# Smaller closings and openings between the attention steps of a four-layer fp32 kernel on one Trainium2 core

## The chip, the cores and the metric

The kernel runs on one core of a Trainium2 chip. The metric is the device time of one execution in microseconds; lower is better. A core has five engines with an instruction queue each: TensorE (PE in the profile; its weight loads are PEld), VectorE (DVE), ScalarE (ACT), GpSimd (POOL) and SyncE (SP), which here only issues DMAs. They work side by side and wait for each other through semaphores. Matmul results go to PSUM, which has eight banks of 512 fp32 values for each of 128 partitions.

## What is computed

The input x is (4, 64, 64, 64) in fp32: four images of 4096 tokens with 64 channels. Four layers follow each other, each with a residual:

```python
# layer 0: self-attention over the 4096 tokens
attn = softmax(q @ k.T); x = gamma * (attn.T @ v) + x
# layer 1: layer norm, 1x1 convolutions, depthwise 3x3, gating, channel attention
# layer 2: attention between the 64 rows of the first spatial axis read as
xf = x.reshape(B, 64, 4096)
scores = einsum('bci,bcj->bij', xf, xf)          # 4096 x 4096, symmetric
out = einsum('bcj,bij->bci', xf, softmax(scores)) + x
# layer 3: non-local block with inner width 32
f = softmax(theta(x) @ phi(x).T); y = f @ g(x)
w_y = y @ w_W + w_b
x = x + gamma * (w_y - mean) * rsqrt(var + eps) + beta   # over all images
```

In layers 0, 2 and 3 each score matrix is 4096 x 4096 for each image, so almost all of the work is matmuls and exponentials.

## The kernel before, in words

x stays in SBUF as the tile `X`, [128, 4 images, 2048]. The program is one list of `items`; `run()` walks it and emits after each item what has become due: `at(i, fn)` puts a function behind item i, and two lanes of generators, `conv` (layer 1) and `misc` (loads, closings, openings), move on as `tick(us)` credits them with time; the number that a generator yields is what it costs its lane. Nothing is scheduled at run time: the engines' queues have the order in which the program emits.

The order of the stages: layer 0 of images 0 to 3 with layer 1 in the `conv` lane; then layer 2 of image 0; then, in turn, layer 2 of image 1, layer 3 of image 0, layer 2 of image 2, layer 3 of image 1, layer 2 of image 3, layer 3 of image 2, layer 3 of image 3.

*PSUM.* In layer 2 `new_ps` hands out slots of two banks (0, 1 and 2 in turn), and `new_acc` the accumulators in banks 6 and 7. In layer 3 `take_banks(7)` lets seven banks go round one at a time; the eighth holds the sum of the products. `new_ps` takes two neighbouring banks there and skips one at the wrap. Scores (L1643) take four of them for each item.

*Layer 2 of image 0* (`layer2`, 32 items) computes all scores. `close2` (L1369-1380) divides by the softmax's sums and adds to X: for each of 4 parts a multiplication (L1377) and an addition (L1379) on VectorE.

*Layer 2 of images 1 to 3* (`layer2s`, 72 items, the "diagonal steps") uses the symmetry. A step `n` computes a block pair of scores (L1432, 8 matmuls), its exponentials (L1437) and the products of a step two back (L1484, 8 matmuls), accumulated in two banks for the block `h` (the order is 7, 0, 1, ... 6) and added to `A` in SBUF (`add_to`, L1474). Blocks off the diagonal are also turned (L1449, a transpose on VectorE), summed by columns on POOL (L1460), and multiplied (`turned_products`, L1500, 128 matmuls into two slots). `weights` sends the rows of x that these need (L1415). `close2s` (L1545-1569) closes such an image in five steps: the sums (L1550-1556), then 4 parts, each with 8 transposes of 128x128 blocks of A (L1561) into one two-bank slot, a multiplication by the reciprocal sums (L1562, 128x1024) and two additions to X (L1568, 128x512 each).

*features2* (L1292-1305) writes the layout `ko` for layer 2's scores: in two groups, 8 transposes (L1300) into one slot, two copies by VectorE and ScalarE (L1303), and a DMA for the other half of the partitions after each (L1304).

*Layer 3* (`open3`, `keys3`, `layer3`). `open3` projects X to theta (L1588), phi (L1599) and g (L1607), each in one two-bank slot, with VectorE adding the biases (L1592, L1603, L1609). `keys3` spreads phi over the partitions by 16 DMAs of SP (L1622). `layer3` has 64 items for each image (two halves `nb` of 32 `mc`): scores L1643, exponentials L1654 in two instructions or more (first bank 0, then banks 1 to 3 as far as they are neighbours), products L1700 two items later. The sums of e over mc are made on VectorE (L1691), and for the eight `mc` in `BY_DMA` by accumulating DMAs of POOL (L1671/L1673), into the tile xn. Four or five items after a half `totals` sums over partitions (L1712) and eleven after it `close` projects (L1750).

*Who closes whom.* Image 0's closing is in the `misc` lane from step 2 of layer 2 of image 1. The closing of images 1 and 2 is at steps 8, 12, 22, 32 and 42 of the next image's layer 2, and the opening of image b-1's layer 3 from step 46. features2 of the next image is in the `misc` lane from item 3 of layer 3 (images 0 and 1). Image 3's closing, opening and keys are in the `misc` lane from item 8 of image 2's layer 3.

Of the kernel before, what the change touches and what calls it, by code (L numbers as in the profile page):

```python
# [691 lines left out]
def fast_path(ctx: ExitStack, tc: tile.TileContext, a: dict, out: bass.AP, bad):  # L692
    nc = tc.nc
# [41 lines left out]

    def take_slots(*slots):
        turn_of["slots"], turn_of["ps"], turn_of["banks"] = list(slots), 0, 0
# [144 lines left out]
    sel4 = const.tile([128, 32], F32, name="sel4")  # L882
    pwb = const.tile([128, 2, 2], F32, name="pwb")
# [22 lines left out]
    def setup():  # L906
# [33 lines left out]
        for i in range(4):  # L940
# [5 lines left out]
            yield 4.0  # L946
        nc.vector.tensor_add(sel4, ident[:, 0:32], ident[:, 32:64])
# [345 lines left out]
    def features2(b):  # L1293
# [3 lines left out]
        for g in range(2):  # L1297
            ps = new_ps()
            for i in range(8):
                nc.tensor.transpose(ps[:, bass.ts(i, 128)], x[:, bass.ts(8 * g + i, 128)], ident)  # L1300
            for e, copy in enumerate((nc.vector.tensor_copy, nc.scalar.copy)):
                own, other = slice(64 * e, 64 * e + 64), slice(64 - 64 * e, 128 - 64 * e)
                copy(kv[own, bass.ts(g, 8), e, :], ps[own, :].rearrange("p (a n) -> p a n", n=128))  # L1303
                nc.sync.dma_start(out=kv[other, bass.ts(g, 8), e, :], in_=kv[own, bass.ts(g, 8), e, :])  # L1304
            yield 7.0

    def layer2(b):
# [7 lines left out]
        def scores(n):  # L1315
# [3 lines left out]
            for jb in range(4 * (n % 8), 4 * (n % 8) + 4):  # L1319
# [13 lines left out]
                conv.tick(2.3)  # L1333
# [53 lines left out]
    def layer2s(b, when_free):  # L1387
# [7 lines left out]
        for h in (7, 0, 1, 2, 3, 4, 5, 6):  # L1395
# [3 lines left out]
                for pi, pair in enumerate(SIDES[h]) for gi, g in enumerate(sorted(pair)) for u in range(2)  # L1399
            ]  # L1400
            steps += other + own if h == 6 else own + other
        st = {"e": {}, "T": {}, "esum": {}}

# [38 lines left out]
        def turned(n):  # L1442
# [3 lines left out]
            if ti == 0 and pi not in st["T"]:  # L1446
                st["T"][pi] = new_big("turned")
            T = st["T"][pi].rearrange("p (e s j) -> p s e j", e=16, s=8)
# [4 lines left out]
        def column_sums(n):  # L1453
# [7 lines left out]
            if (pi, ti) == (1, 3):  # L1461
# [30 lines left out]
        def turned_products(h, pi):  # L1492
            T, slots = st["T"][pi], [new_ps(), new_ps()]
# [11 lines left out]
            for i in range(2):  # L1505
                for gi, g in enumerate(sorted(SIDES[h][pi])):
# [11 lines left out]
        def item(n):  # L1518
            h = steps[n][0]
            if n >= 4 and steps[n - 4][0] == h and (n == 4 or steps[n - 5][0] != h):  # L1520
                weights(h)
# [11 lines left out]
            if n - 2 in last_of:  # L1533
                turned_products(*last_of[n - 2])
                if last_of[n - 2] == (6, 0):
                    when_free()
            if n - 5 in last_of and last_of[n - 5][1] == 1:
# [7 lines left out]
    def close2s(b):  # L1545
        x, m = X[:, b], im[b]
        ps = new_ps()
# [3 lines left out]
        tot = sums2[:, b, :]  # L1551
# [5 lines left out]
        yield 2.0  # L1557
        for i in range(4):
            ps, t = new_ps(), new_t()
            for j in range(8):  # L1560
                nc.tensor.transpose(ps[:, bass.ts(j, 128)], m.A[:, 1024 * i + 128 * j : 1024 * i + 128 * j + 128], ident)  # L1561
            nc.vector.tensor_mul(  # L1562
                t.rearrange("p (j n) -> p j n", n=128), ps.rearrange("p (j n) -> p j n", n=128),
                rz[:, bass.ts(i, 8)].unsqueeze(2).to_broadcast([128, 8, 128]),
            )
            xs = x[:, bass.ts(i, 512)].rearrange("p (j h) -> p j h", h=H)
            for o in range(2):
                nc.vector.tensor_add(xs, xs, t.rearrange("p (j o h) -> p j o h", j=8, o=2)[:, :, o, :])  # L1568
            yield 3.0
# [5 lines left out]
    small = {}  # L1575
    held = []

    def open3(b):
# [4 lines left out]
        ps = new_ps()  # L1583
        for nb in range(2):
            for jj in range(2):
                for s in range(2):
                    k = 2 * s + jj
                    mm(  # L1588
                        ps[32 * k : 32 * k + 32, bass.ts(nb, 512)], thw[64 * s : 64 * s + 64, :],
                        tok(x, s, 2 * nb + jj), start=True, stop=True,  # L1590
                    )
        nc.vector.tensor_scalar_add(m.th, ps, V("L3_conv_theta_b"))  # L1592
        yield 3.5

        ps, own = new_ps(), m.tg[:, 2048:3072].rearrange("p (s n) -> p s n", s=2)
        m.own = own
        for j in range(4):
            for s in range(2):
# [456 lines left out]
```

## Time and profile before

| what | us |
|---|---|
| median of 3 runs | 2469.98 |
| lowest, highest | 2468.93, 2474.80 |
| profiled execution: its own time | 2475.64 |
| profiled execution: its span | 2473.9 |
| PE matmul busy | 2431.5 |
| ACT busy | 1642.7 |
| DVE busy | 1428.7 |
| POOL busy | 506.8 |

The granted clock of TensorE was 0.996 of full speed. The stages that the change touches begin at about: layer 2 of image 0 at 1037, layer 2 of image 1 at 1274, layer 3 of image 0 at 1474, layer 2 of image 2 at 1618, layer 3 of image 1 at 1812, layer 2 of image 3 at 1953, layer 3 of image 2 at 2143, layer 3 of image 3 at 2290.

TensorE's longest waits, as the view of waits gives them for the whole span (what waits, for whom, us in total, how often, the longest):

```profile
PE PS L1484 <- DVE A L1474: 6.1, 1, 6.1
PE PS L1643 <- DVE A L1474: 3.3, 3, 1.5
PE PS L1643 <- ACT e L1654: 2.9, 2, 2.5
```

In a timeline a line has the start, the duration, the engine, the line of the program, the operation, output and input, shapes, and the number of records; what stands in brackets is the time that the engine was idle before, and who ended it. A matmul in fp32 of full weights has two records. Busy time of PE is modelled from starts, and neighbouring groups overlap by a tenth of a microsecond; start to start is the safer reading.

### The profile page before, as it was taken

How to read it: one execution, taken by the hardware profiler on the slowest of the kernel's cores; microseconds unless marked ns; L12 is line 12 of the kernel's file. 1: busy time of each engine (PE TensorE's matmuls, PEld its weight loads, DVE VectorE, ACT ScalarE, POOL GpSimd, SP SyncE). 2: the span in 40 equal slices, each digit the busy share in tenths (PEclk: the TensorE clock that was granted, in tenths of full speed). 3: DMA queues.
4: the chain of work that ended last, by engine and by line, in shares of the span. 5: the costliest groups of instructions: out<-in, count | busy, mean ns of one | idle time of the engine just before them, and what ended most of it. 6: DMA issues, size and time to landing. Idle time of an engine off the chain costs nothing.

```text
span 2473.9 us, 62215 instructions
## 1 busy us (share of the span) xinstructions
PE 2431.5 (98%) x27037; PEld 925.5 (37%) x27037; DVE 1428.7 (58%) x1701; ACT 1642.7 (66%) x2979; POOL 506.8 (20%) x345
## 2 busy tenths in 40 slices
PE   9999999999999999999989999999999999999998
PEld 3343453336433643344324442134431244421123
DVE  2010277228822782267335558877668876687886
ACT  4666766667666766666645459954479744569996
POOL 2000000000000000000007661256631366512110
PEclk9999999999999999999999999999999999999999
DMA  3000000010000000000000027610075400376554
GB/s 79 1 18 1 18 1 18 18 19 1 18 18 18 1 18 18 18 2 18 18 18 19 19 48 151 138 27 21 18 148 116 81 21 22 73 139 127 118 118 119
DMA packets 59151, 115.33 MB, mean 47 GB/s; under 512 B 11149, under 2 KB 30326, under 8 KB 58870
## 3 DMA queue, kind: packets, MB, share of 16 engines
q0 software_dynamic: 19136, 67.68, 13.7%
q1 hardware_dynamic: 38981, 41.75, 7.5%
q8 instruction: 214, 3.51, 0.6%
q10 hardware_dynamic: 752, 1.85, 0.2%
q14 instruction: 68, 0.55, 0.1%
HBM read 4.80 MB, written 4.19 MB: 4 GB/s over the span
## 4 chain that ended last, share of the span: by engine, by line
PE 88%; DVE 5%; ACT 4%; DMA 1%; issue 1%; SPq 0%; POOL 0%; DVEq 0%; ACTq 0%; POOLq 0%
PE PS L1116 18%; PE PS L1090 17%; PE PS L1643 8%; PE PS L1700 8%; PE PS L1432 7%; PE PS L1484 7%; PE PS L1500 6%; PE PS L1323 4%; PE PS L1343 4%; PE PS L1200 2%; DVE tg L1691 2%; ACT e L1654 2%; DMA xn<-e 1%; ACT e L1095 1%; PE PS L1165 1%
## 5 line engine op out<-in xcount | busy, mean ns | idle before, releaser
L1095 ACT ACTIVATE e<-PS 128x1024 f32<-128x1024 f32 x512 | 523.7, 1023 | 331.3 <-PE PS L1090 299.2
L1116 PE MATMUL PS<-e,vq 64*64 64x512 f32 x4096 | 573.8, 591 | 0.0
L1090 PE MATMUL PS<-X,q 64*64 64x512 f32 x4096 | 571.6, 591 | 1.8 <-DVE X L974 1.7
L1654 ACT ACTIVATE e<-PS 128x512 f32<-128x512 f32 (+2 forms) x593 | 500.4, 915 | 66.9 <-PE PS L1643 42.8
L1437 ACT ACTIVATE e<-PS 128x512 f32<-128x512 f32 x432 | 253.5, 594 | 289.6 <-PE PS L1432 270.9
L1691 DVE TENSOR_TENSOR tg<-tg,e 128x2048 f32<-128x2048 f32 x174 | 398.6, 2291 | 49.4 <-ACT e L1654 37.0
L1233 DVE SCALAR_TENSOR_TENSOR y<-pad,vec,y 128x1024 f32<-128x1024 f32 x240 | 308.1, 1284 | 7.5
L1460 POOL TENSOR_TENSOR esum<-esum,e 128x1024 f32<-128x1024 f32 x126 | 298.9, 2372 | 58.6 <-ACT e L1437 51.5
L1643 PE MATMUL PS<-tg,ph 32*64 32x512 f32 x4096 | 300.3, 615 | 6.5 <-DVE A L1474 3.3
L1090 PEld LDWEIGHTS PS<-X,q 64*64 64x64 f32 x4096 | 184.4, 133 | 257.3 <-issue 178.8
L1116 PEld LDWEIGHTS PS<-e,vq 64*64 64x64 f32 x4096 | 184.6, 133 | 251.3 <-issue 152.9
L1700 PE MATMUL PS<-e,tg 128*32 128x512 f32 x2048 | 273.5, 606 | 0.0
L1449 DVE STREAM_TRANSPOSE turned<-e 128x1024 f32<-128x1024 f32 x168 | 206.7, 1239 | 79.8 <-ACT e L1437 79.7
L1484 PE MATMUL PS<-e,X 64*64 64x512 f32 x1728 | 232.7, 594 | 6.2 <-DVE A L1474 6.1
L1432 PE MATMUL PS<-ko 64*64 64x512 f32 x1728 | 235.4, 598 | 0.0
L1528 POOL MEMSET A<- 128x4096 f32 x3 | 11.2, 3736 | 1012.5 <-PE PS L1116 1012.5
L1103 DVE TENSOR_REDUCE sums<-zs 128x1 f32<-128x4 f32 x128 | 19.6, 153 | 301.3 <-ACT e L1095 300.9
L1331 ACT ACTIVATE e<-PS 128x1024 f32<-128x1024 f32 x128 | 129.6, 1023 | 83.7 <-PE PS L1323 80.4
L1500 PE MATMUL PS<-turned,xn 32*64 32x256 f32 x5376 | 157.2, 377 | 2.5 <-DVE sums L1554 1.6
L1673 POOL DMA_DIRECT2D xn<-e x112 | 97.6, 906 | 294.4 <-ACT e L1654 201.1
L1474 DVE TENSOR_TENSOR A<-PS,A 128x256 f32<-128x256 f32 (+1 forms) x216 | 92.5, 477 | 105.2 <-PE PS L1500 80.7
L1643 PEld LDWEIGHTS PS<-tg,ph 32*64 32x64 f32 x4096 | 65.4, 130 | 227.7 <-ACT e L1654 175.8
(224 smaller groups left out, 1927.4 us busy)
## 6 DMA issues: line engine op xcount, KB each, us to landing
xn<-e POOLq DMA_DIRECT2D x128, 512.0 KB, 5.3
xn<-X SPq DMA_DIRECT2D x336, 32.0 KB
xn<-t SPq DMA_DIRECT2D x64, 128.0 KB
ph<-tg SPq DMA_DIRECT2D x64, 128.0 KB
ko<-ko SPq DMA_DIRECT2D x16, 256.0 KB
xr<-in_x_dram SPq DMA_DIRECT2D x13, 256.0 KB
q<-q SPq DMA_DIRECT2D x12, 256.0 KB
out_dram<-o SPq DMA_DIRECT2D x7, 256.0 KB
```

What stands on the lines that cost most here:

```text
L1090: mm(ps[64 * c : 64 * c + 64, bass.ts(r, 512)], m.q[rows_, 128 * t + 64 * c : 128 * t + 64 * c + 64], x[rows_, bass.ts(g, 512)], start=Tru ...
L1095: act(es[g // 2][:, bass.ts(g % 2, 1024)], ps, AF.Exp, bias=SHIFT0, accum_out=zs[:, g : g + 1],)
L1116: ins = mm(PS[64 * s : 64 * s + 64, 2048 + 512 * j : 2560 + 512 * j], vq[rows_, :], es[j // 2][rows_, k : k + 512], start=t == 0 and i < 2 ...
L1233: stt(y1, win, wt, y1, ALU.mult, ALU.add)
L1432: mm(ps[64 * c : 64 * c + 64, bass.ts(r, 512)], m.ko[rows_, k : k + 64], m.ko[rows_, bass.ts(h, 512)], start=True, stop=True,)
L1460: nc.gpsimd.tensor_add(esum, st["e"][n - 1] if (pi, ti) == (0, 1) else esum, st["e"][n])
L1484: mm(st["acc"][r][64 * c : 64 * c + 64, :], xw[rows_, jb, :], st["e"][n][rows_, bass.ts(c, 512)], start=n == mine[0], stop=n == mine[-1],)
L1500: mm(slots[q // 2][64 * c : 64 * c + 64, o : o + 256], st["xr"][rows_, w : w + 64], T[rows_, bass.ts(e, 256)], start=e < 2, stop=e >= 14,)
L1643: mm(PS[64 * c : 64 * c + 64, bass.ts(banks[k], 512)], m.ph[32 * k : 32 * k + 32, 128 * mc + 64 * c : 128 * mc + 64 * c + 64], m.th[32 * k ...
L1654: act(e[:, 512 * lo : 512 * k], PS[:, 512 * banks[lo] : 512 * banks[lo] + 512 * (k - lo)], AF.Exp,)
L1691: nc.vector.tensor_add(esum, esum, e)
L1700: mm(st["y"][32 * k : 32 * k + 32, :], m.gx[:, i % 32, :], es[i][:, bass.ts(k, 512)], start=mc == 0, stop=i % 32 == 31,)
```

## The change

It has seven parts.

1. `piece()` hands out one bank in layer 3. Elsewhere it takes a whole slot and returns its first half.
2. A constant `fold2` (128x64) is two identities of 64 on top of each other. In `close2s` a part is now 8 fp32 matmuls, each with a 128x128 block of A as weights and fold2 as the moving operand, in one bank, followed by 8 fused multiply-adds of 128x64 on VectorE (`stt`: PSUM times the reciprocal sum, plus X). The transposes, the multiplication and the two additions go, and so does the tile `t`.
3. Image 0's closing moves from the `misc` lane at step 2 to steps 12, 13, 22 and 23 of layer 2 of image 1.
4. features2 has 4 pieces of 4 transposes, with half-sized copies and DMAs, twice as many.
5. open3 has 6 one-bank pieces: theta split by half, phi by `s`, g by 8 tokens' groups.
6. `between3` holds what is emitted in layer 3 right after the exponentials of an item: features2 at items 4, 7, 10 and 13; image 3's closing and opening at items 6, 8, ... 26 of image 2's layer 3; its `keys3` behind item 25; `totals` and `close`, except at the end of a half with n = 63 of images 0 and 1. In such an item the exponentials are cut at bank 2 instead of bank 1.
7. In `layer2s`, `weights` of a block is emitted one step before the block begins, T is chosen by a running index, and pairs are taken as `SIDES` gives them. In layer 2 of image 0 `conv.tick` is 2.5 instead of 2.3.

```diff
+    def piece():
+        if turn_of["banks"]:
+            return PS[:, bass.ts(new_bank(), 512)]
+        return new_ps()[:, 0:512]
...
+        nc.vector.tensor_add(fold2, ident[:, 0:64], ident[:, 64:128])
...
-        for g in range(2):
-            ps = new_ps()
-            for i in range(8):
+        for g in range(4):
+            ps = piece()
+            for i in range(4):
...
-                conv.tick(2.3)
+                conv.tick(2.5)
...
         for i in range(4):
-            ps, t = new_ps(), new_t()
+            ps = piece()
             for j in range(8):
-                nc.tensor.transpose(ps[:, bass.ts(j, 128)], m.A[:, 1024 * i + 128 * j : 1024 * i + 128 * j + 128], ident)
-            nc.vector.tensor_mul(
-                t.rearrange("p (j n) -> p j n", n=128), ps.rearrange("p (j n) -> p j n", n=128),
-                rz[:, bass.ts(i, 8)].unsqueeze(2).to_broadcast([128, 8, 128]),
-            )
-            xs = x[:, bass.ts(i, 512)].rearrange("p (j h) -> p j h", h=H)
-            for o in range(2):
-                nc.vector.tensor_add(xs, xs, t.rearrange("p (j o h) -> p j o h", j=8, o=2)[:, :, o, :])
-            yield 3.0
+                c = 1024 * i + 128 * j
+                mm(ps[:, bass.ts(j, 64)], m.A[:, c : c + 128], fold2, start=True, stop=True)
+            for j in range(8):
+                xs = x[:, bass.ts(8 * i + j, 64)]
+                stt(xs, ps[:, bass.ts(j, 64)], rz[:, 8 * i + j : 8 * i + j + 1], xs, ALU.mult, ALU.add)
+            yield
...
-        for j in range(4):
+        for s in range(2):
+            ps = piece()
+            for j in range(4):
+                mm(
+                    ps[32 * j : 32 * j + 32, :], phw[64 * s : 64 * s + 64, :],
+                    tok(x, s, j), start=True, stop=True,
+                )
+            nc.vector.tensor_scalar_add(own[:, s, :], ps, V("L3_conv_phi_b"))
+            yield 3.0
+        for i in range(2):
+            ps = piece()
+            for t in range(8):
+                mm(ps[:, bass.ts(t, 64)], x[:, bass.ts(8 * i + t, 128)], gw, start=True, stop=True)
...
-            exp(0, 1)
+            cut = 2 if first + n in between3 else 1
+            exp(0, cut)
             if mc == 1 and (nb or last):
                 held.append(lambda: exp(1, 4))
             else:
-                exp(1, 4)
+                exp(cut, 4)
+            for fn in between3.get(first + n, []):
+                fn()
...
-                misc_from[f + 2] = [close2(0)]
+                turns = close2(0)
+                for i in (12, 13, 22, 23):
+                    at(f + i, lambda turns=turns: next(turns))
...
-                misc_from[f + 3] = [features2(b + 1)]
+                turns = features2(b + 1)
+                for i in (4, 7, 10, 13):
+                    between3[f + i] = [lambda turns=turns: next(turns)]
...
-    def keys_of_last():
-        keys3(B - 1)
-        yield 3.5
-
-    misc_from[f - 56] = [close2s(B - 1), open3(B - 1), keys_of_last()]
+    ends = [close2s(B - 1)] * 5 + [open3(B - 1)] * 6
+    for i, gen in enumerate(ends):
+        between3[f - 58 + 2 * i] = [lambda gen=gen: next(gen)]
+    at(f - 39, lambda: keys3(B - 1))
```

## The prediction

> **What bounds the kernel now.** I read the page's head first, then the busy time of each engine stage by stage, then TensorE's timeline at the places that the diff touches. The page's head and the shares of the chain of waits:
>
> ```profile
> span 2473.9 us, 62215 instructions
> PE 2431.5 (98%) x27037; PEld 925.5 (37%) x27037; DVE 1428.7 (58%) x1701; ACT 1642.7 (66%) x2979; POOL 506.8 (20%) x345
> PE 88%; DVE 5%; ACT 4%; DMA 1%; issue 1%; SPq 0%; POOL 0%; DVEq 0%; ACTq 0%; POOLq 0%
> ```
>
> TensorE is busy for 2431.5 of 2473.9 us. The view by stretches says the same of the stages that the change touches (us of the stretch, then PE's busy time):
>
> ```profile
> 1290.00:1478.00 188.00, 182.39 (x2976) 86.02 (x2984) 112.21 (x145) 85.46 (x266) 124.23 (x56) 0.98 0.12 30
> 1618.00:1812.00 194.00, 191.79 (x3056) 89.97 (x3048) 130.03 (x166) 92.20 (x287) 125.26 (x56) 1.00 0.13 30
> 2147.00:2290.00 143.00, 139.58 (x1516) 33.41 (x1520) 112.92 (x72) 114.58 (x141) 26.67 (x32) 0.98 0.66 131
> 2290.00:2430.00 140.00, 138.76 (x1609) 27.43 (x1593) 120.16 (x64) 132.00 (x161) 26.64 (x32) 1.00 0.62 124
> ```
>
> These are layer 2 of images 1 and 2, then layer 3 of images 2 and 3. So the sum has two kinds of terms: instructions added to TensorE (each costs its own time) and moments at which TensorE stands still. Two stages hold visible loss. Layer 2 of image 1 is the one with 5.6 us of idle PE and a clock of 0.98; the timeline of its start shows why:
>
> ```profile
> 1286.95 1.04 PE L1432 MATMUL PS<-ko 64*64 64x512 f32 x8
> 1289.39 2.34 POOL L1460 TENSOR_TENSOR esum<-e 128x1024 f32<-128x1024 f32 x1 [256.40 <-ACT e L1437]
> 1289.56 2.71 DVE L1379 TENSOR_TENSOR X<-X,ph 128x512 f32<-128x512 f32 x1
> 1292.19 1.23 DVE L1449 STREAM_TRANSPOSE turned<-e 128x1024 f32<-128x1024 f32 x1
> 1293.36 1.44 DVE L1474 TENSOR_TENSOR A<-PS,A 128x512 f32<-128x512 f32 x2
> 1294.06 4.48 PE L1484 MATMUL PS<-e,X 64*64 64x512 f32 x16 [6.07 <-DVE A L1474]
> 1297.53 2.19 PE L1432 MATMUL PS<-ko 64*64 64x512 f32 x8
> ```
>
> VectorE was still in image 0's closing (L1377/L1379, back to back since 1284.85) when the accumulators had to be added to A (L1474). TensorE waits 6.07 us for them, and the matmuls after it take twice their time: 4.48 us where 16 of them take 1.90, and 2.19 where 8 take 1.04.
>
> Layer 3 of image 2 carries image 3's closing and opening. TensorE's timeline there:
>
> ```profile
> 2163.64 1.09 PE L1561 MATMUL PS<-ident,A 128*128 128x128 f32 x8
> 2175.44 2.31 PE L1643 MATMUL PS<-tg,ph 32*64 32x512 f32 x16
> 2192.52 3.79 PE L1607 MATMUL PS<-gw,X 128*128 128x64 f32 x32
> 2197.23 1.11 PE L1643 MATMUL PS<-tg,ph 32*64 32x512 f32 x16
> 2224.69 1.98 PE L1643 MATMUL PS<-tg,ph 32*64 32x512 f32 x6 [2.48 <-ACT e L1654]
> ```
>
> The scores of an item take 1.11 us; the 2.31 at 2175.44 means that they waited inside for a bank. And in layer 2 of image 3, where image 2's opening stands between steps:
>
> ```profile
> 1737.69 1.04 PE L1484 MATMUL PS<-e,X 64*64 64x512 f32 x8
> 1738.66 1.09 PE L1599 MATMUL PS<-X,phw 64*32 64x512 f32 x16
> 1739.68 1.09 PE L1432 MATMUL PS<-ko 64*64 64x512 f32 x8
> 1740.59 1.04 PE L1484 MATMUL PS<-e,X 64*64 64x512 f32 x8
> ```
>
> Start to start, the phi matmuls (L1599) take 1.02 there.
>
> **What the Trainium skill says.** "TensorEngine Tiling (Array Packing)", Key Properties: changing the tiling mode drains TensorE. The trace agrees: score to product is 0.86 us start to start, but 0.97 before such an insertion and 0.91 after it (the lines above), so a switch there and back is 0.16. "TensorE: Matmul & The Clock Gate", Terms: the transpose mode is four times faster for fp32; and under LDWEIGHTS, a weight load's time goes with its columns. The trace shows transposes of 128x128 at 0.128 us each (L1561, 8 in 1.02) and fp32 matmuls with 128-column weights and 64 moving columns at 0.2325 (L1607, 16 in 3.72; by the groups its weight loads are busy for 14.6 us in the four images, 3.65 each): not four times, but the second kind does cost more. The same page, "What's actually happening": an idle window of some 3.4 us drops the clock to half. Here 6.07 and 2.48 us of idle PE were followed by doubled matmuls. "SBUF — State Buffer", "SBUF: two separate sides": VectorE with two SBUF inputs and GpSimd lock each other out. The trace agrees: L1379 takes 0.69 alone and 2.71 beside POOL's L1460.
>
> **The change, part by part** (against the profiled execution's span).
>
> *Fold instead of transposes (layer 2 of images 2 and 3).* Each of 4 parts: 8 transposes, 1.02 us, become 8 fp32 matmuls with the A block as 128x128 weights and 64 moving columns. The nearest row is L1607: 8 x 0.2325 = 1.86. That is +0.84 a part; TensorE has no other slack, so 8 parts give +6.7. Bounds: +6.0 (matmuls overlap somewhat better) to +8.5 (the slot, one of three in layer 2, is held by VectorE longer). VectorE: before 1.22 + 2 x 0.69 to 0.935; after 8 fused operations of 128x64, whose nearest rows take 0.21 to 0.29 each, so 1.8 to 2.3. Nothing gained or lost there, since TensorE bounds and the next part comes 10 items later.
>
> *Image 0's closing moved to items 12, 13, 22, 23.* The 6.07 us of idle and the half clock at 1294 go, except that the A add still comes after the first turn (L1449) of the fourth step: at the same place in image 2, 1.17 us went from score to product instead of 0.91, with another matmul covering 1.0 of it. So some 1.5 to 2.1 us of waiting stay. Lost now: 6.07 + 2.5 = 8.6 (the 2.5 is what the slow matmuls took beyond their own time). I take -6.3, with -4 to -8.6. At the new places the pieces (1.4 us each alone) fall around block 0's adds to A (four in 1.42 us); VectorE is busy there for 112 of 188 us, and TensorE notices a late add only when the bank it frees comes round again.
>
> *open3 in six one-bank pieces, in layer 2 of images 1, 2 and 3.* In layer 2 a "bank" is still a whole slot of three. L1588: 8 matmuls in two rounds, 1.86, same work. L1599: 8 matmuls in one round, 1.02; split by s only one of the two row halves works at a time, so two pieces of 1.02: +1.02. One more mode switch, 0.16, for each of phi and the g part, and a wait for a slot of about 0.2. Sum +1.5 for each image, +4.5; 3 to 7.
>
> *features2 in pieces of 4.* In layer 0 and in layer 2 of image 0: two more mode switches each, some +0.4 and +0.4. In layer 3 (images 0 and 1): 8 transposes of 1.02 become two of about 0.55 each; the two stalls of 0.5 and 0.2 us at the old insertions, where the scores waited for the copies, shrink, but there are four places. +0.8 over both, -1.5 to +3. SP gets 8 DMAs of half the size instead of 4; SP has little queued there and ko is needed only 140 us later: nothing.
>
> *Image 3 in layer 3 of image 2.* Before: from 2161.40 to 2197.23 are 11 items, 35.83 us, of which 11 x 2.04 = 22.44 is the items' own; 13.4 on top: matmuls 11.3 and bank stalls 2.1. Then keys3's DMAs, which SP sends from about 2191, met the accumulating DMAs of mc 17, 20 and 23 (9 to 10.5 us instead of 5.3):
>
> ```profile
> ACT e L1654 <- DMA xn<-e: 5.7, 2, 3.9
> ```
>
> ACT waited 5.7 us for them, PE 0.39 and 2.48, and four groups at half clock: 8.0 us in all. Together 21.4. After: matmuls 0.35 + 4 x 1.86 + 2.04 + 2 x 1.02 + 2 x 1.86 = 15.6, one bank each, at every second item, with the exp of that item cut into two halves; stalls of some 0.2 at each of 11 places = 2.2. keys3's DMAs start when the second phi piece is done (item 22, not 18), so that only mc 23 still meets them; one late transfer holds one of the six e buffers, where three held three, and I count nothing. 17.8 - 21.4 = -3.6. Bounds: -8 (no stalls, mode switches hidden) to +2 (the collision costs 6 us still).
>
> *Totals and close between the exps; conv.tick 2.5; weights issued a step earlier in the program; T's index.* Instruction order on POOL and SP is the same, on ACT and DVE nearly; the waits that bound totals (ACT's held exp) stay. 0, -2 to +1.
>
> Sum: 0.8 + 6.7 - 6.3 + 4.5 + 0.8 - 3.6 + 0 = +2.9. The profiled execution took 2475.64 us, 1.7 more than its span of 2473.9, and would become 2478.5; it lies 5.7 above the median of the runs, 2469.98, so the forecast on the median's footing is 2472.9.
>
> **Rivals.**
> (a) *Both losses vanish whole and the fold overlaps.* Start of image 1 -8.6, layer 3 of image 2 -8, features2 -1.5, totals -2, fold only +6, open3 +3, the small +0.8: -10.3, so 2459.7. For it: the losses are measured. Against it: the fold is bound by weight loads (L1607's loads take 3.65 of 3.72), and slots still rotate among three. 0.15.
> (b) *Slower: TensorE's added work and held slots in layer 2.* Everything there stands on the path: fold +8.5, open3 +7, the start of image 1 only -4, layer 3 of image 2 -1, the small terms +2: +12.5, so 2482.5. It decides from the point at which VectorE's eight small operations keep a slot for more than the 2.6 us in which the scores come back to it; they then delay TensorE at each of 8 + 18 insertions by half a microsecond. For it: 98% of PE is busy, so nothing hides work. Against it: VectorE is at 60%. 0.33.
> (c) *The collision moves with the keys.* As forecast, but keys3 at item 22 meets mc 23 and mc 2 of the next half: +6, so 2478.9. Its chance is inside (b).
> (d) *The change doesn't do what it says*, the closing meets POOL's adds at its new place as well and waits 2.71 us a piece: TensorE waits again, -2 instead of -6.3, 2477.2. Inside the forecast's range.
>
> **How the numbers follow.** The forecast, 2472.9, has 0.52; (a) 0.15; (b) with (c) 0.33. The range goes from 2463 to 2484: the forecast's own range, 2465 to 2480, and (b) as well as the upper half of (a). A measurement of this kernel tells about 0.3%, 7.4 us, from no change: under 2462.6 is faster, over 2477.4 slower. Of the forecast's cases nearly all fall in between, of (a)'s most are faster, of (b)'s nine in ten slower: 0.14, 0.52, 0.34.
>
> **What would show it.** The fold's eight matmuls at 1.86 a part in layer 2, or else the price was wrong. At the start of image 1 PE's wait before the first products: about 2 us and no doubled matmuls. The phi pieces at 1.02 each. In layer 3 of image 2 matmuls of 15.6 us and no wait of ACT for xn. If PE's busy sum rises by less than 12 us or the stalls at one-bank insertions exceed 0.5 us each, the sum is wrong.

## The result: 0.5% slower

| | kernel before | changed kernel |
|---|---|---|
| median, us | 2473.57 (6 runs, 2468.93 to 2474.80) | 2484.61 (6 runs, 2484.30 to 2485.78) |
| profiled execution: its time | 2475.64 | 2484.51 |
| profiled execution: its span | 2473.9 | 2482.7 |

The ratio is 1.005, with a 95% interval of [1.0037, 1.0063]. The forecast was 2472.9 with a range to 2484.0; the measured time is above that range, near rival (b)'s 2482.5, but not for (b)'s reason. The forecast stood on 2469.98, the median of three runs of the kernel before; with six runs this median is 2473.57, so 3.6 us of the distance belong to the baseline and not to the change. Against the six runs the change cost 11.0 us where +2.9 was forecast.

The head of the page of the changed kernel, and the shares of its chain of waits:

```profile
span 2482.7 us, 62533 instructions
PE 2444.4 (98%) x27133; PEld 930.9 (37%) x27133; DVE 1416.1 (57%) x1786; ACT 1643.9 (66%) x2980; POOL 507.3 (20%) x345
PE 89%; DVE 5%; ACT 4%; issue 1%; DMA 0%; DVEq 0%; SPq 0%; ACTq 0%
```

TensorE is as full as before, with 12.9 us more of busy time. A table by stage tells where the time went. A stage runs from the first score of its layer and image to the first score of the next stage, in the order of the program; the times are read from TensorE's timelines.

| stage | before | changed | difference | forecast |
|---|---|---|---|---|
| layers 0 and 1 | 1016.47 | 1017.24 | +0.8 | +0.4 |
| layer 2, image 0 | 257.80 | 262.55 | +4.75 | +0.4 |
| layer 2, image 1 | 199.55 | 191.96 | -7.6 | -4.8 |
| layer 3, image 0 | 137.60 | 137.90 | +0.3 | +0.4 |
| layer 2, image 2 | 197.10 | 202.13 | +5.03 | +4.85 |
| layer 3, image 1 | 137.98 | 137.90 | -0.1 | +0.4 |
| layer 2, image 3 | 197.10 | 202.13 | +5.03 | +4.85 |
| layer 3, image 2 | 156.31 | 157.29 | +1.0 | -3.6 |
| layer 3, image 3, and the end | 173.95 | 173.64 | -0.3 | 0 |

Two rows are far worse than forecast: layer 2 of image 0 by 4.35 us, and layer 3 of image 2 by 4.6. Layer 2 of image 1 is 2.8 us better, of which 1.9 is work that moved from there into layer 2 of image 0 (see the run with features2 and the tick undone). The rest is within 0.5 us. Together that makes the 6.0 us by which the profiled execution missed its forecast.

One stage also differs between executions of the same code: layer 2 of image 1 took 191.96 us here and in one other run, and 193.65 in three others that don't touch it. The last section shows why.

TensorE's waits in layer 3 of image 2, in the changed kernel (who waits for whom, us in total, how often, the longest); the kernel before had 2.9 us there for ScalarE, none for tg:

```profile
PE PS L1725 <- DVE tg L1704: 3.4, 1, 3.4
PE PS L1653 <- DVE A L1485: 0.9, 1, 0.9
```

and its timeline at that wait, which is at `totals` of the first half:

```profile
2241.29 1.57 PE L1653 MATMUL PS<-tg,ph 32*64 32x512 f32 x16
2246.27 1.94 PE L1725 MATMUL PS<-tg,ones 128*32 128x512 f32 x8 [3.41 <-DVE tg L1704]
2247.95 1.96 PE L1713 MATMUL PS<-e,tg 128*32 128x512 f32 x8
2249.84 1.95 PE L1653 MATMUL PS<-tg,ph 32*64 32x512 f32 x16
2251.72 1.06 PE L1713 MATMUL PS<-e,tg 128*32 128x512 f32 x8
```

The three groups after the wait take 1.9 us instead of 1.07 to 1.11, and the granted clock says the same. In the view by stretches the second number is the length in us and the third from the right, in front of the DMA's two, the clock:

```profile
2244.77:2251.60 6.83, 5.33 (x32) 1.01 (x32) 4.52 (x4) 0.20 (x1) 0.00 (x0) 0.50 0.35 136
2251.60:2254.00 2.40, 2.40 (x36) 0.55 (x32) 2.21 (x2) 2.17 (x4) 0.00 (x0) 1.00 0.00 0
```

Before, the wait of ScalarE for xn cost TensorE time in this stage; now TensorE waits for VectorE. VectorE's timeline in the changed kernel shows where it becomes late:

```profile
2212.66 2.28 DVE L1704 TENSOR_TENSOR tg<-tg,e 128x2048 f32<-128x2048 f32 x1
2218.05 0.75 DVE L1619 TENSOR_TENSOR tg<-PS,bc_L_conv_g_b 128x256 f32<-128x256 f32 x2 [3.11 <-ACT e L1664]
2218.73 2.28 DVE L1704 TENSOR_TENSOR tg<-tg,e 128x2048 f32<-128x2048 f32 x1
2224.06 0.75 DVE L1619 TENSOR_TENSOR tg<-PS,bc_L_conv_g_b 128x256 f32<-128x256 f32 x2 [3.06 <-ACT e L1664]
2224.74 9.47 DVE L1704 TENSOR_TENSOR tg<-tg,e 128x2048 f32<-128x2048 f32 x4
2234.24 2.29 DVE L1706 TENSOR_TENSOR tg<-tg,xn 128x2048 f32<-128x2048 f32 x1
2236.64 9.48 DVE L1704 TENSOR_TENSOR tg<-tg,e 128x2048 f32<-128x2048 f32 x4
```

Twice VectorE stands idle for 3.1 us at a bias addition of the g pieces (L1619, items 24 and 26), although the sum addition queued behind it (L1704) has its e. The brackets name ScalarE, but g's matmuls on TensorE, which the addition reads, end at nearly the same moment: those of item 26 run from 2221.96 to 2223.96, and ScalarE's exponential of that item ends at 2224.06. Which of the two came last is not told apart here. Either way the bias addition waits for work of its own item, and the sum addition behind it, which could run, waits with it. The addition for mc 24 starts 3.8 us after the scores of item 26; in layer 3 of image 1, with nothing inserted there, the same addition starts 1.0 us ahead of them. After mc 24 no time is made good. Eight additions of 2.37 us start to start and one of xn follow without gaps, and TensorE needs only 2.04 us for an item. L1725 starts at 2246.27, as soon as the last addition is done.

### The profile page after: what moved, and what is told of

Its sections match the earlier page's. It is cut to its first block, busy times and chain, and to the rows that moved or that the text cites. A ratio compares the mean times of both kernels' runs of the same rounds, so it can differ in the third digit from the quotient of the medians.

```text
span 2482.7 us, 62533 instructions
## 1 busy us (share of the span) xinstructions
PE 2444.4 (98%) x27133; PEld 930.9 (37%) x27133; DVE 1416.1 (57%) x1786; ACT 1643.9 (66%) x2980; POOL 507.3 (20%) x345
## 4 chain that ended last, share of the span: by engine, by line
PE 89%; DVE 5%; ACT 4%; issue 1%; DMA 0%; DVEq 0%; SPq 0%; ACTq 0%
PE PS L1123 17%; PE PS L1097 17%; PE PS L1653 9%; PE PS L1713 8%; PE PS L1442 7%; PE PS L1495 7%; PE PS L1511 6%; PE PS L1350 4%; PE PS L1330 4%; DVE tg L1704 3%; PE PS L1207 2%; ACT e L1664 2%; PE PS L1574 1%; ACT e L1102 1%; PE PS L1172 1%
## 5 line engine op out<-in xcount | busy, mean ns | idle before, releaser
L1704 DVE TENSOR_TENSOR tg<-tg,e 128x2048 f32<-128x2048 f32 x174 | 398.4, 2289 | 42.9 <-ACT e L1664 31.4
L1653 PE MATMUL PS<-tg,ph 32*64 32x512 f32 x4096 | 295.3, 614 | 2.8 <-DVE A L1485 2.7
L1460 DVE STREAM_TRANSPOSE turned<-e 128x1024 f32<-128x1024 f32 x168 | 206.6, 1238 | 86.3 <-ACT e L1447 86.3
L1511 PE MATMUL PS<-turned,xn 32*64 32x256 f32 x5376 | 157.2, 377 | 2.5 <-DVE sums L1566 1.6
```

The source lines that it names most:

```text
L1511: mm(slots[q // 2][64 * c : 64 * c + 64, o : o + 256], st["xr"][rows_, w : w + 64], T[rows_, bass.ts(e, 256)], start=e < 2, stop=e >= 14,)
L1653: mm(PS[64 * c : 64 * c + 64, bass.ts(banks[k], 512)], m.ph[32 * k : 32 * k + 32, 128 * mc + 64 * c : 128 * mc + 64 * c + 64], m.th[32 * k ...
L1704: nc.vector.tensor_add(esum, esum, e)
```

## The experiments

Each is one edit on the changed kernel, if nothing else is said; the ratio is to runs of the kernel before on the same chip.

**The g pieces early** (e1_g_early). Image 3's opening gets another order: only the two g pieces move, from items 24 and 26 to 15 and 17, so that VectorE's queue is free of g's bias additions from item 18 on:

```diff
-    for i, gen in enumerate(ends):
-        between3[f - 58 + 2 * i] = [lambda gen=gen: next(gen)]
+    for i, gen in zip((6, 8, 10, 12, 14, 15, 16, 17, 18, 20, 22), ends):
+        between3[f - 64 + i] = [lambda gen=gen: next(gen)]
...
+        early = [(g, 0), (theta, 0), (g, 1), (theta, 1), (phi, 0), (phi, 1)]
```

> The changed kernel with image 3's opening in another order: the two g pieces at items 15 and 17 of image 2's layer 3, theta at 16 and 18, phi at 20 and 22 as before. Theory (VectorE's queue): the bias additions of the g pieces at items 24 and 26 stand in VectorE's queue ahead of the sum additions and hold them back by nearly 4 us, which is the 3.41 us that TensorE waits at totals, and the half clock after it costs another 2.6. Then the wait falls to at most 0.6 us, no matmul is doubled, layer 3 of image 2 goes from 157.3 us to about 151.5, and the time from 2484.6 to about 2479. Rival (lost cover): before the change the delay by the DMA collision gave VectorE the time that it needs; with TensorE on time the wait comes wherever the g pieces stand. Then the wait stays at some 3 us and the time at 2484.

Measured: 2479.08 us, ratio 1.0026 [1.0016, 1.0036]; the stage took 151.75 us. TensorE's timeline at totals:

```profile
2242.22 1.57 PE L1658 MATMUL PS<-tg,ph 32*64 32x512 f32 x16
2244.05 1.07 PE L1730 MATMUL PS<-tg,ones 128*32 128x512 f32 x8 [0.26 <-ACT e L1669]
2244.94 1.04 PE L1718 MATMUL PS<-e,tg 128*32 128x512 f32 x8
```

and VectorE's:

```profile
2219.90 2.29 DVE L1709 TENSOR_TENSOR tg<-tg,e 128x2048 f32<-128x2048 f32 x1 [0.46 <-ACT e L1669]
2222.47 9.48 DVE L1709 TENSOR_TENSOR tg<-tg,e 128x2048 f32<-128x2048 f32 x4 [0.28 <-ACT e L1669]
2231.99 2.29 DVE L1711 TENSOR_TENSOR tg<-tg,xn 128x2048 f32<-128x2048 f32 x1
```

The wait of 3.41 us is 0.26, no matmul there is doubled, and the stage is 5.54 us shorter. The theory of VectorE's queue holds with its number. The rival of the lost cover is refuted: ScalarE waited only 0.7 us for xn, and the wait at totals did not come back.

**Transposes again in layer 2** (images 1 and 2; image 3 keeps the fold):

```diff
+            if b < B - 1:
+                ps, t = new_ps(), new_t()
+                for j in range(8):
+                    nc.tensor.transpose(ps[:, bass.ts(j, 128)], m.A[:, 1024 * i + 128 * j : 1024 * i + 128 * j + 128], ident)
...
+                yield
+                continue
             ps = piece()
```

> The changed kernel with the old closing (8 transposes, a multiplication, two additions) for images 1 and 2, whose closings lie in layer 2; image 3 keeps the fold. Theory (price of the fold): 4 parts x 0.905 us of TensorE time fall away in each of two stages, so layer 2 of images 2 and 3 go from 202.1 to about 198.5 each and the time from 2484.6 to about 2477.4. Rival (held slots): the added time is waiting for a slot that VectorE's eight small operations hold; then the matmuls' sum falls by the same 0.905 a part and TensorE's idle time falls too, over 1 us a stage, and the time goes to 2475 or less.

Measured: 2477.24 us, ratio 1.0019 [1.0012, 1.0026]; layer 2 of images 2 and 3 took 198.52 us each, 3.61 less. By start to start in TensorE's timelines 7.71 us of fold matmuls in a stage became 4.09 of transposes, and TensorE's gaps stayed (1.24 and 1.21 us at L1511). So the cost is the matmuls' price and not held slots. The view of groups, of the changed kernel and then of the kernel before, shows how much of the time weights are loaded (PEld):

```profile
L1574 PE MATMUL PS<-fold,A 128*128 128x64 f32 x192 | 24.0, 278 | 0.2
L1574 PEld LDWEIGHTS PS<-fold,A 128*128 128x128 f32 x192 | 22.3, 191 | 10.1 <-issue 7.5 <-ACT e L1664 2.6
L1561 PE MATMUL PS<-ident,A 128*128 128x128 f32 x96 | 13.1, 280 | 0.0
L1561 PEld LDWEIGHTS PS<-ident,A 128*128 128x128 f32 x96 | 10.3, 141 | 9.8 <-issue 8.1 <-DVE t L1562 0.8 <-ACT e L1654 0.8
```

Of 24.0 us of fold matmuls (12 parts, so 2.0 a part with the overlap) weights are loaded in 22.3; for the transposes of 12 parts it is 10.3 of 13.1. This fits a price that the weight loads set, but no run separates the loads from the matmuls.

**Image 0's closing back at step 2** (e3_close0_back):

```diff
-                turns = close2(0)
-                for i in (12, 13, 22, 23):
-                    at(f + i, lambda turns=turns: next(turns))
+                misc_from[f + 2] = [close2(0)]
```

> The changed kernel with image 0's closing back in the misc lane at step 2. Theory (VectorE late for A): the wait of about 6 us for the addition to A and the half clock after it come back; layer 2 of image 1 goes from 192.0 us to about 198 and the time to about 2490.6. Rival (the tail of layer 1): the stage is 7.6 us shorter mostly since layer 1's last matmuls and VectorE work left it with conv.tick 2.5; then the wait comes back with less than 3 us and the time stays under 2487.

Measured: 2487.49 us, ratio 1.0056 [1.0039, 1.0073]; layer 2 of image 1 took 195.0 us. Neither expectation holds to the letter. The wait for A came back with 3.2 us, where the kernel before has 6.1, and the median is 2.9 us above the changed kernel's; that is just outside what the rival allowed. These are 4 runs from 2483.61 to 2488.67, and the stage is 3.0 us longer than in the changed kernel's profile but 1.3 longer than in the runs with 193.65, so the 2.9 is rough. The reason is in the last run below.

**features2 and conv.tick as before outside layer 3:**

```diff
-                conv.tick(2.5)
+                conv.tick(2.3)
...
+        w = 4 if turn_of["banks"] else 8
+        for g in range(16 // w):
+            ps = piece() if w == 4 else new_ps()
```

> The changed kernel with features2 of images 0 and 1 in two pieces of 8 transposes and conv.tick 2.3 as before; in layer 3 features2 keeps its four pieces. Theory: layer 2 of image 0 became 4.75 us longer through 2.1 us of layer 1's tail that moved in, 1.7 us of waiting for a slot that ScalarE's copy of ko held, and the rest mode switches and half clock; so the stage goes back to about 258, layer 2 of image 1 gets 1.9 us of it back, and the time goes from 2484.6 to about 2482. Rival (a mere shift of the tail): the sum of the two stages stays at 454.5 us within 0.5, and so does the time.

Measured: 2480.86 us, ratio 1.0034 [1.0023, 1.0046]. Layer 2 of image 0 went back by 4.74 us to 257.81, and layer 2 of image 1 got 2.13 longer than in the changed kernel's profile, 194.08. By start to start 1.87 us of that is layer 1's last matmuls (1.01 + 0.86). So the two stages together are 2.6 us shorter, the rival of a mere shift falls, and the time fell by 3.75 us where 2.6 was expected. TensorE's timeline of the changed kernel shows the longest wait among the loss:

```profile
1154.48 0.66 PE L1307 MATMUL PS<-ident,X 128*128 128x128 f32 x4
1155.07 2.01 PE L1330 MATMUL PS<-ko 64*64 64x512 f32 x16
1158.82 0.66 PE L1363 MATMUL PS<-ident,ph 128*128 128x128 f32 x4 [1.74 <-ACT ko L1310]
```

The transposes of `turn` (L1363) wait 1.74 us for the slot of a features2 piece, which ScalarE's copy to ko still held. The run undid both edits at once, so it does not tell the pieces from the tick.

**Phi whole in layer 2:** the phi projection of images 0 to 2 in one two-bank piece of 8 matmuls, as before the change.

```diff
+        if not turn_of["banks"]:
+            ps = new_ps()
+            for j in range(4):
+                for s in range(2):
...
-        for s in range(2):
+        for s in range(2 if turn_of["banks"] else 0):
             ps = piece()
```

> The changed kernel with phi in one piece of 8 matmuls in a two-bank slot where open3 lies in layer 2 (images 0 to 2); image 3's stays split. Theory (two row halves work at once): each of the three stages of layer 2 gets 0.97 us shorter, 192.0 or 193.6 to about 191 or 192.6 and 202.1 to 201.2, and the time goes from 2484.6 to about 2481.7. Rival (the slot wait is what costs): the matmuls' time stays and only 0.1 us of waiting goes, so the time stays within 0.5.

Measured: 2480.96 us, ratio 1.0035 [1.0022, 1.0047]. In layer 2 of image 2 phi's matmuls went from 1.99 us to 1.02, as the theory has it. The stage itself got only 0.46 us shorter, to 201.67, and the layer 3 that follows another 0.44. The time fell by 3.65 us where 2.9 was expected; 1.4 us of this is in the profile of layer 3 of image 2, whose opening the edit doesn't change; the half clock after the wait at totals lasted 3.41 us there in place of 6.83. The changed kernel's timeline has the two pieces, of 1.0 us each, although they have half the matmuls:

```profile
1740.66 1.06 PE L1608 MATMUL PS<-X,phw 64*32 64x512 f32 x8
1741.65 1.09 PE L1442 MATMUL PS<-ko 64*64 64x512 f32 x8
1742.56 1.04 PE L1495 MATMUL PS<-e,X 64*64 64x512 f32 x8
1743.53 1.06 PE L1608 MATMUL PS<-X,phw 64*32 64x512 f32 x8
1744.52 1.09 PE L1442 MATMUL PS<-ko 64*64 64x512 f32 x8
```

**Everything together** (e6_mixed): the old closing and opening in layer 2, features2 in two pieces outside layer 3, conv.tick 2.3, g early. What remains of the change is mainly image 0's closing, the fold for image 3, and the one-bank insertions in layer 3.

> Parts of both kernels: the changed one with the old closing and the old three-piece opening in layer 2, features2 in two pieces outside layer 3, conv.tick 2.3, and image 3's g pieces at items 15 and 17. Theory (the terms add up): 2484.6 - 5.5 (g early) - 7.3 (transposes) - 3.7 (features2 and tick) - 2.9 (phi) - 0.4 (g in one piece) = 2464.8, some 8 us faster than the kernel before. Rival (the savings overlap, since a delay in one place is cover in another): at most half of it, 2475.

Measured: 2464.86 us, ratio 0.9967 [0.9954, 0.9979]. The terms add up within a microsecond, and the mix is faster than both kernels. That the sum came out to a tenth is luck: it had phi at 2.9 us, and with the measured 3.65 it would be about 2464.

**No fold at all.** The mix, with image 3's closing in eight one-bank pieces, each followed by a multiplication of 128x512 and two additions of 128x256:

```diff
-            for j in range(8):
-                c = 1024 * i + 128 * j
-                mm(ps[:, bass.ts(j, 64)], m.A[:, c : c + 128], fold2, start=True, stop=True)
+            for q in range(2):
+                ps, t = piece(), new_t()
+                for j in range(4):
+                    c = 1024 * i + 512 * q + 128 * j
+                    nc.tensor.transpose(ps[:, bass.ts(j, 128)], m.A[:, c : c + 128], ident)
...
+                yield
```

> e6_mixed with image 3's closing by transposes too, in eight one-bank pieces of 4 transposes, a multiplication of 128x512 and two additions of 128x256, at items 7 to 14. Theory (TensorE's time counts): 7.7 us of fold become 4.1 of transposes and 0.5 of mode switches, so 3 us less than e6_mixed, about 2462. Rival (VectorE's time counts there): VectorE has some 4 us more to do and doesn't catch up before the end of the half, the wait at totals comes back, and the time is e6_mixed's or more.

Measured: 2462.40 us, ratio 0.9957 [0.9941, 0.9974]. This is the fastest of the study, though its lead over the mix (2.5 us, intervals overlapping) rests on 4 runs. The profiled execution, 2464.29 us, is the slowest of the four, and in it the stage got only 0.34 us shorter: fold matmuls of 7.68 us became 4.69 us of transposes, but a wait for ScalarE of 1.23 us and a half clock of 3.41 us, which the mix's profile doesn't have, took most of it back. In that execution ScalarE waited for xn:

```profile
ACT e L1726 <- DMA xn<-e: 2.7, 1, 2.7
```

**Where do the long transfers of xn come from, and what do they cost?** Four runs. First (e7_keys_early), on the order of the run with g early, phi first and the keys behind item 17, then g and theta up to item 22:

```diff
-        early = [(g, 0), (theta, 0), (g, 1), (theta, 1), (phi, 0), (phi, 1)]
+        early = [(phi, 0), (phi, 1), (g, 0), (g, 1), (theta, 0), (theta, 1)]
...
-    at(f - 39, lambda: keys3(B - 1))
+    at(f - 47, lambda: keys3(B - 1))
```

> The order of e1_g_early, but phi first (items 15 and 16), then g (17 and 18), then theta (20 and 22), with the keys' DMAs sent behind item 17. Theory (collision on the DMA queues): the keys meet the accumulating DMAs of mc 17, 20 and 23 again, ScalarE waits some 5 us for xn, TensorE loses 6 to 8 us, and the time goes from e1_g_early's 2479.1 to 2485 or more. Rival (the keys' place doesn't matter, the two-bank insertions did it): no wait of ScalarE for xn and a time within 1 us of 2479.

Measured: 2479.26 us, ratio 1.0025 [1.0015, 1.0036]. The transfers of xn were stretched to 11.6 us, and ScalarE did not wait for them. So the theory's cost did not come, and the rival's time did; but its reason is not shown, since the transfers were long. A long transfer and a cost are two things. Second, the same with everything inserted up to item 20 and the keys behind item 16:

```diff
-    for i, gen in zip((6, 8, 10, 12, 14, 15, 16, 17, 18, 20, 22), ends):
+    for i, gen in zip((6, 8, 10, 12, 14, 15, 16, 17, 18, 19, 20), ends):
...
-    at(f - 47, lambda: keys3(B - 1))
+    at(f - 48, lambda: keys3(B - 1))
```

> e7_keys_early with nothing inserted behind the keys: phi at items 15 and 16, g at 17 and 18, theta at 19 and 20, keys sent behind item 16. Theory (collision and pitch): in e7_keys_early the transfers of xn were stretched to 11.6 us as before the change, but the insertions at items 17 to 22 made the items long, so the six e buffers did not run out; with pure items of 2.04 us from item 21 on ScalarE waits for xn again, 2 us or more, and the time is 2 to 5 us above e7_keys_early's 2479.3. Rival (no cost from the keys at all): no wait for xn, and a time within 1 us of 2479.

Measured: 2479.33 us, ratio 1.0026 [1.0016, 1.0035]. The wait came, with 2.2 us, and the stage was 1.0 us longer in the profile (152.73 against 151.71), but the time did not rise by the 2 us or more. TensorE waited only 0.2 us for ScalarE. The part of the expectation on the time failed; at most the direction is shown.

Third, on the kernel before, the keys moved in the program behind item 28:

```diff
-    misc_from[f - 56] = [close2s(B - 1), open3(B - 1), keys_of_last()]
+    misc_from[f - 56] = [close2s(B - 1), open3(B - 1)]
+    at(f - 36, lambda: keys3(B - 1))
```

> The kernel before, with one edit: image 3's keys are sent behind item 28 of image 2's layer 3 instead of item 18 or so, past the accumulating DMAs of the half. Theory (the collision cost 8 us that can be had back): ScalarE's wait for xn and the doubled matmuls go, layer 3 of image 2 goes from 156.3 us to about 149, and the time from 2472.5 to about 2465. Rival (it was cover for VectorE): TensorE then waits at totals for the sums, 3 us and a half clock, so the stage stays above 153 us and the time above 2469.

Measured: 2472.93 us, ratio 1.0003 [0.9994, 1.0011]. The edit moved nothing: SyncE sends the keys as soon as phi is there, and the first left 47.3 us after the stage's start in both kernels. So the run says nothing about either theory, but it is a second profile of what is in effect the kernel before. There ScalarE waited

```profile
ACT e L1654 <- DMA xn<-e: 3.7, 2, 2.4
```

for xn and the stage took 151.44 us, where the profile behind the prediction has 5.7 us and 156.31. The profiled executions took 2469.39 us, at the low end of their runs, and 2475.64, above all six of its own. The last run below has the stage in the same order too, with a wait for xn of 6.2 us and 155.46. So the loss that the prediction set at 8.0 us differs by 5 from one execution to the next; 8.0 is the high end of the three.

Fourth, phi itself was moved, in the kernel before, behind item 26, and the keys with it:

```diff
+        if b < B - 1:
+            phi_of(b)
+            yield 3.5
...
+    at(f - 38, lambda: (phi_of(B - 1), keys3(B - 1)))
```

> The kernel before, with image 3's phi projection taken out of its place (item 16 or so) and put behind item 26 of image 2's layer 3, so that the keys' DMAs, which SyncE sends as soon as phi is there, can't start before the last accumulating DMA of the half. Theory (keys stretch the accumulating DMAs, by a different amount in each execution): the DMAs of xn take at most 9 us, ScalarE doesn't wait for them, the spread of the runs shrinks from 8 us to 2, and the time is 2466 to 2470. Rival (VectorE has no time to give): VectorE's sum additions, held back by phi's bias addition, make TensorE wait at totals by 2 us or more, and the time stays within 2 us of the kernel before, with the small spread.

Measured: 2471.24 us, ratio 0.9993 [0.9985, 1.0002]. Here no keys met the accumulating DMAs of the first half, none of these took over 7.1 us (10.5 in the kernel before), ScalarE never waited for xn, and the runs lie in 3.1 us, where the kernel before spread over 6.8. Yet the time is the same within the interval, for the rival's reason:

```profile
PE PS L1717 <- DVE tg L1696: 2.5, 1, 2.5
```

TensorE waits at totals for the sums, which phi's bias addition (L1588) held back. VectorE's timeline shows it idle 2.0 us ahead of that addition; a moment earlier it had still been waiting for ScalarE, so it was not late:

```profile
2208.79 2.29 DVE L1696 TENSOR_TENSOR tg<-tg,e 128x2048 f32<-128x2048 f32 x1 [1.43 <-ACT e L1659]
2213.07 1.28 DVE L1588 TENSOR_SCALAR tg<-PS,vec 128x1024 f32<-128x1024 f32 x1 [1.99 <-PE PS L1584]
2214.27 7.08 DVE L1696 TENSOR_TENSOR tg<-tg,e 128x2048 f32<-128x2048 f32 x3
```

The 2.0 us of waiting and the 1.28 us of the addition cover the 2.5 us. It is the changed kernel's fault, put into the kernel before by one moved piece.

**Image 0's closing alone** at its new steps, in the kernel before:

```diff
-                misc_from[f + 2] = [close2(0)]
+                turns = close2(0)
+                for i in (12, 13, 22, 23):
+                    at(f + i, lambda turns=turns: next(turns))
```

> The kernel before with one part of the change alone: image 0's closing at steps 12, 13, 22 and 23 of image 1's layer 2. Theory (VectorE late for A, with layer 1's tail still in the stage): TensorE's wait of 6.1 us falls to about 1.3 and the doubled matmuls go, layer 2 of image 1 from 199.55 to about 193, and the time falls by 6.5 us, to about 2466.3. Rival (the tail of layer 1 holds VectorE back as much): less than 3 us, as in e3_close0_back.

Measured: 2466.86 us, ratio 0.9974 [0.9964, 0.9983]: faster by 5.5 us. The stage took 192.65 us, 6.9 less. The view of waits there:

```profile
PE PS L1484 <- DVE A L1474: 1.2, 1, 1.2
```

With the run that put the closing back, this answers what that one left open. With layer 1's tail in the stage the move is worth 6.9 us of it; with the tail gone (conv.tick 2.5) the old place costs only 3.0 against the changed kernel's profile. VectorE's timelines show the difference. In the kernel before the closing's first multiplication starts 10.6 us after the stage's start, and its last addition takes 2.71 us beside POOL's L1460. In the run with the closing back it comes 7.9 us after the stage's start, and its last addition takes 0.69 us and is over when POOL's sum has just begun. So the tick and the move saved partly the same wait.

## Why the prediction was wrong

*The steps that held.* The fold was set at +0.84 a part and measured +0.905 (3.62 in four parts). open3 was set at +1.5 an image; phi's +0.97, g's +0.14 and the rest make 1.4 of the stage's 5.03. The start of layer 2 of image 1 left a wait of 1.3 us where 1.5 to 2.1 was said, and moving the closing was worth 6.9 us there where 6.3 was said.

*The step that failed first* is "17.8 - 21.4 = -3.6" for layer 3 of image 2, and in it the sentence "stalls of some 0.2 at each of 11 places = 2.2". It is not the stalls: these were even smaller. In the changed kernel the 21 items with insertions took 59.35 us, 16.5 over their own 21 x 2.04, of which the matmuls are 15.6. But the sum priced TensorE's insertions alone. It did not ask what is late next when the stall for xn goes, and the term for totals set at 0 what then came: "the waits that bound totals (ACT's held exp) stay". The wait at totals of this half was 0.3 us for ScalarE before and 3.41 us for VectorE after. Each insertion also puts an operation into VectorE's queue, one that waits for TensorE, ahead of the sum additions. Placed at items 24 and 26, where from mc 24 on VectorE needs 2.37 us for each item of 2.04, 3.8 us could not be made good. It cost 5.5 us (the run with g early), and the run with phi late shows it from the other side. The profile before had a sign of it. TensorE waited for VectorE at totals four times, half a microsecond in the layer 3 of images 0 and 1 each, so VectorE had nothing to spare there:

```profile
PE PS L1712 <- DVE tg L1691: 2.2, 4, 0.6
```

*The second* is the same sum's "Together 21.4". The 8.0 us in it were read from one execution. Of three profiles with this order in the stage it is the costliest, and the cheapest has a stage 4.9 us shorter. Against the median the excess is smaller: the profiled execution lies 2.1 us above the median of its six runs, which is the difference between the 11.0 us of the medians and the 8.9 of the profiled executions. The forecast took a gain from the upper end of a spread and then set it against a median, and that median, of three runs, was itself 3.6 us too low.

*The third* is the 0 for conv.tick together with +0.4 for features2 in layer 2 of image 0. The stage got 4.75 us longer, of which 1.9 only moved over from the next. Undoing both was worth 3.75 us of the time (the run with features2 and the tick undone). The prediction named no wait there. The runs show one of 1.74 us, for a slot that `turn` needs and that ScalarE's copy to ko still holds; how the loss divides between the pieces and the tick stays open.

*The rivals.* (b) forecast 2482.5 by slots held in layer 2; the time came near, the mechanism did not: the run with transposes left TensorE's gaps as they were. (c) did not come: with the keys behind item 22 ScalarE did not wait for xn in the changed kernel's profile, and 0.7 and 1.3 us in the run with g early and in the mix, without a stall of TensorE over 0.3 us. (d) came by half: at the new place two of the four parts of the closing were slow on VectorE (up to 2.64 us for a multiplication and 1.65 for an addition, 0.68 and 0.69 in the other parts), but TensorE did not wait for them.

## What to carry to other kernels

An insertion is priced on every engine whose queue it enters: what stands behind its waiting instruction, and how much slack that engine has before the next point at which somebody waits for its total. Where VectorE needs more time for an item than TensorE, as from mc 24 on here, a delay is not made good; work for VectorE goes ahead of such a stretch. A stall seen in one profiled execution should be compared with the spread of the runs before it is written down as a gain.

## What the runs showed of the hardware

*The half clock comes in steps.* In the traces' record of the granted clock the stretches at 0.50 are 3.41 or 6.83 us long, 16 of them in 14 profiles (the end of each program, where TensorE has little to do, left aside). The same wait was followed by one or the other. After the wait of 3.41 us at totals the clock was halved for 6.83 us in the changed kernel and two of its variants, which cost 2.4 to 2.6 us beyond the wait (three groups, start to start, against 2.90 us in the run with g early), and for 3.41 us in two others, which cost 1.4 and 1.6; the run with transposes in layer 2 is one of these:

```profile
2239.27:2242.68 3.41, 2.92 (x16) 0.68 (x16) 1.20 (x3) 0.00 (x0) 0.00 (x0) 0.50 0.39 155
2242.68:2246.00 3.32, 3.32 (x44) 0.62 (x40) 3.22 (x2) 1.82 (x2) 0.00 (x0) 1.00 0.02 5
```

After the wait of 1.30 us at the start of layer 2 of image 1 there was no half clock in two runs of the same code and one of 3.41 us in three, and that is their 191.96 and 193.65 us. So a wait far under the 3.4 us that the prediction spoke of can be followed by it, and the cost of one wait differs by up to 1.7 us from one execution to the next. It is part of the spread of the stage with the keys as well: 6.83, 3.41 and 0 us of half clock in the profiles with 156.31, 155.46 and 151.44 us.

*Row halves.* Phi split by row halves took as long for 4 matmuls on one half (1.0 us) as for 8 on both (1.02).

*Transfers.* Beside the keys' DMAs single transfers of xn took up to 10.5 us in the kernel before and 11.9 in the run with no fold. Without keys beside them they took at most 7.1 in the first half of the run with phi late, and up to 8.1 in the changed kernel.

*Weights.* A matmul of 64 moving columns with 128-column fp32 weights cost 0.24 us, with weights being loaded for nearly all of it, against 0.128 for a transpose of twice the columns.
